# Attention's projection in two halves, its result added by ScalarE and GpSimd, and part of the layer norm's scale and shift on ScalarE

## The chip, the cores and the metric

The kernel runs on one core of a Trainium2 chip. The core has five engines that run side by side, each with its own queue of instructions, and that wait for one another through semaphores: TensorE (PE in the profile, its weight loads apart as PEld), VectorE (DVE), ScalarE (ACT), GpSimd (POOL) and SyncE (SP). Matrix products land in PSUM, a memory of eight banks; one bank holds one tile of 128 x 512 float32 numbers. Everything else lies in the larger SBUF. The metric is the time of one execution on the device in microseconds (us), the median of several runs.

## The reference, cut to what matters

The network takes an image of 256 x 256 positions with 32 channels through four layers, each a group norm, a layer and a residual addition. The change is in the first layer, attention over an axis of length one:

```
B, s, i, _ = m.shape
mn = (m - mu) * jax.lax.rsqrt(var + LN_EPS) * ln_gamma + ln_beta
v = (mn @ Wv).reshape(B, s, i, H, C)
g = jax.nn.sigmoid(mn @ Wg).reshape(B, s, i, H, C)
a = jax.nn.softmax(a, axis=2)
...
o = g * jnp.einsum('bstih,bsihc->bsihc', a, v)
o = o.reshape(B, s, i, H * C)
return o @ Wo + bo
...
x = x + _L0_conv_ref(_gn(x), ...)
```

The softmax runs over an axis of length one and is 1, so the layer is `x + (sigmoid(mn @ Wg) * (mn @ Wv)) @ Wo + bo`, with `mn` the layer norm of the group-normed image. Two edge-filter layers and a recurrent layer over 256 time steps follow.

## The kernel before

The image lies in SBUF as `xa`, 128 partitions by 64 blocks by 256 columns: four neighbouring positions of 32 channels each fill the partitions. Two blocks make a pair of 128 x 512 numbers, and there are 32 pairs. `xb` holds the layer norm's result in the same form.

The layer norm ends with a loop over the 32 pairs. For each, TensorE spreads the reciprocal deviation over the partitions into a PSUM tile `pb` (L252, the pool `ps_sp` with eight banks), VectorE multiplies the pair by it (L259), and GpSimd multiplies by `gamma4` and adds `beta4` (L260). Here a scheduler keeps the program's order on each engine; the three run as a pipeline.

Attention follows, in pools of its own: `ps_g` with four banks, `ps_v` with four. They take the PSUM of the layer norm's pools, so their first tile waits for the last reader there. The work is cut into 64 units, two for each pair: unit `u = 2i + half` of step `i` computes one half of the 256 hidden columns for pair `i`.

- `gate(u)`: four matmuls (L277), one for each of the four positions, each with 32 rows of weights and 512 columns, each into its own bank of `ps_g`; then ScalarE takes the sigmoid of each into SBUF tiles `sg` (L288).
- `value(u)`: four matmuls (L277) into the four banks of `ps_v`; then VectorE multiplies each by its `sg` into `o` (L296).
- `project(i)`: eight matmuls (L302), four for each half of the hidden columns, which sum into one bank of `ps_g`, 32 of its partitions for each position. VectorE adds this sum, the bias `bo4` and the residual in one instruction (L310), and takes the statistics for the next group norm (L311).

A float32 matmul is recorded as two instructions, so four of them stand as x8 in the trace. The four matmuls of a gate or value group use different rows of TensorE and run together.

The order on each engine is the order in which the code is written (`tc.manual_schedule`). A step has `value(2i)`, `gate(2i+1)`, `value(2i+1)`, `gate(2i+2)` and `project(i-1)`: gates are one unit ahead of values, and the projection is one step behind. A tile's matmul waits until the earlier reader of its bank is done: the ScalarE sigmoid or VectorE's addition for `ps_g`, VectorE's product for `ps_v`.

After the last step the group norm of the second layer takes the statistics together (L140), and everything later waits for that.

Of the kernel before, what the change touches and what calls it, by code (L numbers as in the profile page):

```python
# [10 lines left out]
F32 = mybir.dt.float32  # L11
AF = mybir.ActivationFunctionType
ALU = mybir.AluOpType
# [3 lines left out]
S = 256  # L17
T = 256
C = 32
J = 4  # L20
NB = T // J
P = 128
# [36 lines left out]
def net_kernel(  # L59
# [20 lines left out]
    nc = tc.nc  # L80
# [11 lines left out]
    xa = big.tile([P, NB, S], F32, name="xa")  # L92
    xb = big2.tile([P, NB, S], F32, name="xb")
# [15 lines left out]
    def per_channel(v, name):  # L109

        t = cp.tile([P, 1], F32, name=name)
        for j in range(J):
            nc.gpsimd.dma_start(out=t[j * C : (j + 1) * C, :], in_=v.rearrange("(c o) -> c o", o=1))
        return t

    gamma4 = per_channel(ln_gamma, "gamma4")
    beta4 = per_channel(ln_beta, "beta4")
    bo4 = per_channel(b_o, "bo4")
# [10 lines left out]
    wo = cp.tile([P, D // P, C], F32, name="wo")  # L129
    nc.gpsimd.dma_start(out=wo, in_=w_o.rearrange("(k p) c -> p k c", p=P))  # L130

    NST = NB // 2

    def new_stats():
        return small.tile([P, NST, nc.vector.BN_STATS_DIM], F32, name="stats")
# [24 lines left out]
    stats = new_stats()  # L160
    WL = 32
    with tc.tile_pool(name="nat", bufs=3) as natp, tc.tile_pool(
        name="ps_in", bufs=4, space=PSUM
    ) as ps_in:
        for w0 in range(0, T, WL):
# [3 lines left out]
            for b2 in range(WL // (2 * J)):  # L169
# [10 lines left out]
                dst = xa[:, blk : blk + 2, :].rearrange("p b s -> p (b s)")  # L180
# [13 lines left out]
    pairs = [(g * KS + ks, g, ks) for ks in range(KS) for g in range(4)]  # L194

    def pair(t, k):
        return t[:, 2 * k : 2 * k + 2, :].rearrange("p b s -> p (b s)")

    with tc.tile_pool(name="ln", bufs=4) as lnp:


        avg = lnp.tile([P, KS, KS, J], F32, name="avg", bufs=1)
        nc.gpsimd.memset(avg, 0.0)
        for ks in range(KS):
            nc.gpsimd.tensor_copy(avg[:, ks, ks, :], kt[:, K_AVG, 0:P:C])
        spread = lnp.tile([P, KS * J, C], F32, name="spread", bufs=1)
        for g in range(4):
            rows = slice(g * C, (g + 1) * C)
            nc.gpsimd.tensor_copy(
                spread[rows], ident[rows, rows].unsqueeze(2).to_broadcast([C, KS * J, C])  # L210
            )
        rstd = lnp.tile([P, 2 * S], F32, name="rstd", bufs=1)
        with tc.tile_pool(name="ps_ln", bufs=6, space=PSUM) as ps_ln, tc.tile_pool(
            name="ps_var", bufs=1, space=PSUM
        ) as ps_var:
            cen = lnp.tile([P, P], F32, name="cen", bufs=1)
            nc.vector.tensor_scalar(cen, kt[:, K_CEN, :], gn[0], None, ALU.mult)
            pcb = ps_var.tile([P, 1], F32, name="pcb")
            nc.tensor.matmul(pcb, lhsT=kt[:, K_CEN, :], rhs=gn[1], start=True, stop=True)
            cb = lnp.tile([P, 1], F32, name="cb", bufs=1)  # L220
            nc.vector.tensor_copy(cb, pcb)
            pvar = ps_var.tile([P, 2 * S], F32, name="pvar")
            sqs = {}

            def variance(k, g, ks):
                nc.tensor.matmul(
                    pvar[g * C : (g + 1) * C, :],
                    lhsT=avg[:, ks].rearrange("p k j -> p (k j)"),
                    rhs=sqs.pop(k),
                    start=ks == 0,  # L230
                    stop=ks == KS - 1,
                )

            for i, (k, g, ks) in enumerate(pairs):
                pc = ps_ln.tile([P, 2 * S], F32, name="pc")
                nc.tensor.matmul(pc, lhsT=cen, rhs=pair(xa, k), start=True, stop=True)
                sqs[k] = lnp.tile([P, 2 * S], F32, name="sq", bufs=10)
                nc.scalar.activation(sqs[k], pc, AF.Square, bias=cb)
                nc.vector.tensor_scalar(pair(xb, k), pc, cb, None, ALU.add)
                if g == 3 and ks:  # L240
                    for q in pairs[i - 7 : i - 3]:
                        variance(*q)
            for q in pairs[-4:]:
                variance(*q)
            std = lnp.tile([P, 2 * S], F32, name="std", bufs=1)
            nc.scalar.activation(std, pvar, AF.Sqrt, bias=ln_eps)
            nc.vector.reciprocal(rstd, std)
        with tc.tile_pool(name="ps_sp", bufs=8, space=PSUM) as ps_sp:
            for k, g, ks in pairs:
                rows = slice(g * C, (g + 1) * C)  # L250
                pb = ps_sp.tile([P, 2 * S], F32, name="pb")
                nc.tensor.matmul(  # L252
                    pb,
                    lhsT=spread[rows, ks * J : (ks + 1) * J, :].rearrange("p j c -> p (j c)"),
                    rhs=rstd[rows, :],
                    start=True,
                    stop=True,
                )
                nc.vector.tensor_mul(pair(xb, k), pair(xb, k), pb)  # L259
                nc.gpsimd.tensor_scalar(  # L260
                    pair(xb, k), pair(xb, k), gamma4, beta4, ALU.mult, ALU.add
                )

    stats = new_stats()
    with tc.tile_pool(name="at", bufs=3) as atp, tc.tile_pool(
        name="ps_g", bufs=4, space=PSUM
    ) as ps_g, tc.tile_pool(name="ps_v", bufs=4, space=PSUM) as ps_v:
        gates, gated = {}, {}  # L270

        def inner(w, u, j, ps):
            i, half = divmod(u, 2)
            k = pairs[i][0]
            rows = slice(j * C, (j + 1) * C)
            mn = xb[rows, 2 * k : 2 * k + 2, :].rearrange("p b s -> p (b s)")
            nc.tensor.matmul(  # L277
                ps, lhsT=w[rows, half * P : (half + 1) * P], rhs=mn, start=True, stop=True
            )
            return ps  # L280

        def gate(u):
            pgs = [
                inner(wg4, u, j, ps_g.tile([P, 2 * S], F32, name="pg")) for j in range(J)
            ]
            for j, pg in enumerate(pgs):
                gates[u, j] = sg = atp.tile([P, 2 * S], F32, name="sg", bufs=8)
                nc.scalar.activation(sg, pg, AF.Sigmoid)  # L288

        def value(u):  # L290
            pvs = [
                inner(wv4, u, j, ps_v.tile([P, 2 * S], F32, name="pv")) for j in range(J)
            ]
            for j, pv in enumerate(pvs):
                gated[u, j] = o = atp.tile([P, 2 * S], F32, name="o", bufs=17)
                nc.vector.tensor_mul(o, pv, gates.pop((u, j)))  # L296

        def project(i):
            po = ps_g.tile([P, 2 * S], F32, name="pg")
            for half in range(2):  # L300
                for j in range(J):
                    nc.tensor.matmul(  # L302
                        po[j * C : (j + 1) * C, :],
                        lhsT=wo[:, half, :],
                        rhs=gated.pop((2 * i + half, j)),
                        start=half == 0,
                        stop=half == 1,
                    )
            dst = pair(xa, pairs[i][0])
            nc.vector.scalar_tensor_tensor(dst, po, bo4, dst, ALU.add, ALU.add)  # L310
            nc.vector.bn_stats(stats[:, i, :], dst)  # L311

        with tc.manual_schedule():
            gate(0)
            for i in range(NST):
                value(2 * i)
                gate(2 * i + 1)
                value(2 * i + 1)
                if i + 1 < NST:
                    gate(2 * i + 2)  # L320
                if i >= 1:
                    project(i - 1)
            project(NST - 1)
    with tc.tile_pool(name="ps_gn", bufs=1, space=PSUM) as ps_gn:
        gn = group_norm(stats, ps_gn)

# [549 lines left out]
```

## Time and profile before

The time before is 3012.37 us, the median of three runs between 3011.68 and 3013.71. The profiled execution spans 3003.6 us.

| stretch of the span | us | what runs |
|---|---|---|
| 0 to 40 | 40 | load, transposes, first statistics |
| 40 to 83 | 43 | group norm, centring and variance of the layer norm |
| 88 to 108 | 20 | scale by the deviation (32 products on VectorE), scale and shift on GpSimd |
| 107.4 to 360.1 | 253 | attention |
| 360 to 655 | 295 | two edge-filter layers |
| after | 2349 | weights and recurrence |

| instruction of the trace | count | mean ns |
|---|---|---|
| L288 ScalarE, sigmoid of 128 x 512 from PSUM | 256 | 602 |
| L296 VectorE, product with `sg` from PSUM | 256 | 678 |
| L310 VectorE, sum with bias and residual | 32 | 751 |
| L311 VectorE, statistics | 32 | 694 |
| L260 GpSimd, scale and shift of 128 x 512 | 32 | 776 |

A line of the timeline has the start in us, the length in us, the engine, the source line, the operation, the tile written and the tiles read, their shapes, and how many instructions were merged; in brackets stand the idle time of the engine before and what ended it. A line of the waits has the waiting engine, tile and line, then whom it waited for, the sum in us, the number of times, and the longest. A line of the stages has the stretch, its length, each engine's busy time with the number of instructions, and the clock that TensorE was granted (1.00 is full). Ends of matmuls are modelled, so a busy TensorE may still stand idle, and instructions that follow each other closely overlap, so that 678 ns products can start 0.6 us apart.

### The profile page before, as it was taken

The numbers are of one execution on the slowest core, as the hardware profiler recorded it, in microseconds if no ns is written. First come the engines' busy times: TensorE is split into PE (matmuls) and PEld (weight loads), VectorE is DVE, ScalarE is ACT, GpSimd is POOL, SyncE is SP. The second block draws the span as 40 slices with busy tenths as digits, with TensorE's granted clock in tenths as the row PEclk, the third lists the DMA queues.
The fourth block names the chain that finished last, engine by engine and source line by source line (L and its number), as shares of the span: only waits on it lengthen the run. The fifth ranks groups of instructions, "written<-read, shape, count | busy, mean of one in ns | idle before, by whom it ended". The sixth has DMA issues, their size and how long they took to land.

```text
span 3003.6 us, 39237 instructions
## 1 busy us (share of the span) xinstructions
PE 2830.3 (94%) x10209; PEld 1042.6 (35%) x10209; DVE 2646.4 (88%) x6572; ACT 1986.9 (66%) x5393; POOL 1718.6 (57%) x2272
## 2 busy tenths in 40 slices
PE   7899898988999999999999999999999999999997
PEld 4433333332333333333333333333333333333332
DVE  5778798986999999999999999999999999999997
ACT  5355486755666666676666766676666666666665
POOL 2300055636666666666666666666666666666665
PEclk9899999988999999999999999999999999999999
DMA  3000000001000000000000000000000000000000
GB/s 128 1 1 1 1 1 1 1 15 24 11 16 8 15 9 15 8 15 8 15 8 15 8 16 7 17 15 8 16 8 15 10 16 8 16 8 15 1 8 9
DMA packets 29314, 38.42 MB, mean 13 GB/s; under 512 B 5732, under 2 KB 22149, under 8 KB 29080
## 3 DMA queue, kind: packets, MB, share of 16 engines
q1 hardware_dynamic: 27392, 33.57, 3.9%
q8 instruction: 84, 1.38, 0.2%
q10 hardware_dynamic: 888, 1.95, 0.2%
q14 instruction: 150, 1.23, 0.1%
q0 software_dynamic: 800, 0.30, 0.0%
HBM read 10.63 MB, written 8.39 MB: 6 GB/s over the span
## 4 chain that ended last, share of the span: by engine, by line
PE 42%; DVE 39%; POOL 10%; issue 4%; ACT 2%; DVEq 0%; POOLq 0%; ACTq 0%
DVE ve L731 13%; PE zz L718 11%; POOL rs L734 9%; DVE zn L738 8%; PE zz L713 7%; DVE c L759 6%; DVE c L767 6%; PE pv L277 4%; PE pt L777 4%; PE pg L440 4%; PE pg L400 3%; PE px L792 2%; PE zz L702 2%; PE pg L302 2%; DVE h L774 2%
## 5 line engine op out<-in xcount | busy, mean ns | idle before, releaser
L734 POOL TENSOR_TENSOR rs<-ve,mhalf 128x4 f32<-128x4 f32 x1024 | 1036.6, 1012 | 281.5 <-DVE ve L731 237.1
L718 PE MATMUL zz<-wc,hT 128*128 128x512 f32 x2040 | 962.6, 594 | 1.2 <-DVE hT L782 1.2
L754 ACT ACTIVATE ga<-zn 128x384 f32<-128x384 f32 x1024 | 531.3, 519 | 468.0 <-DVE zn L738 467.5
L738 DVE TENSOR_TENSOR zn<-zz,rs 128x512 f32<-128x512 f32 x1024 | 701.1, 685 | 84.7 <-POOL rs L734 76.6
L763 POOL TENSOR_TENSOR fc<-ga,c 128x128 f32<-128x128 f32 x1020 | 466.8, 458 | 522.4 <-ACT ga L754 522.4
L731 DVE TENSOR_REDUCE ve<-sq 128x4 f32<-128x516 f32 x1024 | 697.2, 681 | 16.6 <-POOL sq L669 14.1
L726 ACT ACTIVATE sq<-zz 128x512 f32<-128x512 f32 x1024 | 606.3, 592 | 26.6 <-PE zz L718 14.3
L702 PE MATMUL zz<-fx,xt 33*128 33x512 f32 x2048 | 584.8, 643 | 11.5 <-DVE zn L738 8.2
L713 PE MATMUL zz<-wc,hT 128*128 128x512 f32 x1024 | 525.3, 595 | 0.0
L718 PEld LDWEIGHTS zz<-wc,hT 128*128 128x128 f32 x2040 | 359.6, 196 | 264.6 <-DVE hT L782 213.7
L771 ACT ACTIVATE th<-c 128x128 f32<-128x128 f32 x1024 | 311.4, 304 | 182.6 <-DVE c L767 177.9
L777 PEld LDWEIGHTS pt<-ident,h 128*128 128x128 f32 x1024 | 141.9, 139 | 804.8 <-DVE h L774 710.2
L777 PE MATMUL pt<-ident,h 128*128 128x128 f32 x1024 | 321.7, 314 | 87.6 <-DVE h L774 79.2
L767 DVE TENSOR_TENSOR c<-c,fc 128x128 f32<-128x128 f32 x1020 | 291.2, 286 | 55.9 <-DVE c L759 2.3
L759 DVE TENSOR_TENSOR c<-ga 128x128 f32<-128x128 f32 x1024 | 302.9, 296 | 38.7 <-ACT ga L756 38.6
L756 ACT ACTIVATE ga<-zn 128x128 f32<-128x128 f32 x1024 | 303.2, 296 | 0.0
L774 DVE TENSOR_TENSOR h<-ga,th 128x128 f32<-128x128 f32 x1024 | 292.0, 285 | 0.8 <-ACT th L771 0.8
L702 PEld LDWEIGHTS zz<-fx,xt 33*128 33x128 f32 x2048 | 156.1, 185 | 298.4 <-PE zz L718 226.3
L288 ACT ACTIVATE sg<-pg 128x512 f32<-128x512 f32 x256 | 132.1, 602 | 110.8 <-PE pg L277 110.8
L713 PEld LDWEIGHTS zz<-wc,hT 128*128 128x128 f32 x1024 | 183.3, 219 | 2.3 <-issue 2.3
L393 POOL TENSOR_TENSOR dh<-pp 128x512 f32<-128x512 f32 x64 | 99.4, 1553 | 115.6 <-DVE pp L380 98.9
L296 DVE TENSOR_TENSOR o<-pv,sg 128x512 f32<-128x512 f32 x256 | 155.4, 678 | 4.4 <-ACT sg L288 4.1
(147 smaller groups left out, 2306.8 us busy)
## 6 DMA issues: line engine op xcount, KB each, us to landing
xt<-xa SPq DMA_DIRECT2D x256, 64.0 KB, 2.0
nat<-in_x_dram SPq DMA_DIRECT2D x16, 512.0 KB, 8.3
out_dram<-st SPq DMA_DIRECT2D x32, 256.0 KB, 2.3
wc<-in_L_conv_W_cell_dram ACTq DMA_DIRECT2D x2, 512.0 KB, 4.1
kt<-in_consts_dram ACTq DMA_DIRECT2D x1, 832.0 KB
wv<-in_L_conv_Wv_dram POOLq DMA_DIRECT2D x4, 32.0 KB, 4.8
wg<-in_L_conv_Wg_dram POOLq DMA_DIRECT2D x4, 32.0 KB, 6.6
gamma<-in_L_conv_ln_gamma_dram POOLq DMA_DIRECT2D x4, 0.1 KB, 6.1
```

Source lines behind the costliest of these rows:

```text
L702: nc.tensor.matmul(zz, lhsT=x, rhs=fx[rows, l, :], start=True, stop=l == 0 and t == 0)
L713: nc.tensor.matmul(get("zz"), lhsT=v["hT", 0, t][:, seqs], rhs=wc[:, l, 0, :], start=False, stop=t == 0)
L718: nc.tensor.matmul(get("zz"), lhsT=v["hT", l, t - 1][:, seqs], rhs=wc[:, l, 1, :], start=False, stop=True,)
L726: nc.scalar.activation(sqs[l, h][:, :, 0:H], four(get("zz")), AF.Square, scale=float(H**-0.5))
L731: nc.vector.tensor_reduce(ve, sqs[l, h], AX.X, ALU.add)
L734: nc.gpsimd.tensor_tensor(rs, get("ve"), mhalf, ALU.pow)
L738: nc.vector.tensor_mul(four(zn), four(get("zz")), get("rs").unsqueeze(2).to_broadcast([P, 4, H]))
L754: nc.scalar.activation(ga[:, 0 : 3 * H], get("zn")[:, 0 : 3 * H], AF.Sigmoid)
L759: nc.vector.tensor_mul(c, gates(get("ga"), 0), gates(get("ga"), 3))
L763: nc.gpsimd.tensor_mul(fc, gates(get("ga"), 1), get("c"))
L767: nc.vector.tensor_add(c, c, get("fc"))
L777: nc.tensor.transpose(pt[:, 0:P], get("h"), ident)
```

## The change

`project` is called twice for a step. The first call, before `value(2i+1)`, opens the sum in a bank of `ps_g` with the first half's four matmuls; the second, after `gate(2i+2)`, adds the other four. It is meant to fill TensorE between the other groups and to take work from VectorE: the finished sum goes through ScalarE, which adds the bias and writes it to an SBUF tile `r`, and GpSimd adds `r` to the residual. The statistics stay on VectorE, in a function of their own that is called three steps later, so that VectorE need not wait for GpSimd. In the layer norm, 12 of the 32 scale-and-shift operations (groups 1 and 3, where `ks % 4 < 3`) go from GpSimd to ScalarE, so that the two share them.

```diff
                 nc.vector.tensor_mul(pair(xb, k), pair(xb, k), pb)
-                nc.gpsimd.tensor_scalar(
-                    pair(xb, k), pair(xb, k), gamma4, beta4, ALU.mult, ALU.add
-                )
+                if g % 2 and ks % 4 < 3:
+                    nc.scalar.activation(
+                        pair(xb, k), pair(xb, k), AF.Identity, scale=gamma4, bias=beta4
+                    )
+                else:
+                    nc.gpsimd.tensor_scalar(
+                        pair(xb, k), pair(xb, k), gamma4, beta4, ALU.mult, ALU.add
+                    )
...
-        def project(i):
-            po = ps_g.tile([P, 2 * S], F32, name="pg")
-            for half in range(2):
-                for j in range(J):
-                    nc.tensor.matmul(
-                        po[j * C : (j + 1) * C, :],
-                        lhsT=wo[:, half, :],
-                        rhs=gated.pop((2 * i + half, j)),
-                        start=half == 0,
-                        stop=half == 1,
-                    )
-            dst = pair(xa, pairs[i][0])
-            nc.vector.scalar_tensor_tensor(dst, po, bo4, dst, ALU.add, ALU.add)
-            nc.vector.bn_stats(stats[:, i, :], dst)
+        sums = {}
+
+        def project(i, half):
+            if half == 0:
+                sums[i] = ps_g.tile([P, 2 * S], F32, name="pg")
+            for j in range(J):
+                nc.tensor.matmul(
+                    sums[i][j * C : (j + 1) * C, :],
+                    lhsT=wo[:, half, :],
+                    rhs=gated.pop((2 * i + half, j)),
+                    start=half == 0,
+                    stop=half == 1,
+                )
+            if half == 1:
+                r = atp.tile([P, 2 * S], F32, name="r", bufs=2)
+                nc.scalar.activation(r, sums.pop(i), AF.Identity, bias=bo4)
+                dst = pair(xa, pairs[i][0])
+                nc.gpsimd.tensor_add(dst, dst, r)
+
+        def statistics(i):
+            nc.vector.bn_stats(stats[:, i, :], pair(xa, pairs[i][0]))
 
         with tc.manual_schedule():
             gate(0)
             for i in range(NST):
                 value(2 * i)
                 gate(2 * i + 1)
+                if i >= 3:
+                    statistics(i - 3)
+                if i >= 1:
+                    project(i - 1, 0)
                 value(2 * i + 1)
                 if i + 1 < NST:
                     gate(2 * i + 2)
                 if i >= 1:
-                    project(i - 1)
-            project(NST - 1)
+                    project(i - 1, 1)
+            for half in range(2):
+                project(NST - 1, half)
+            for i in range(NST - 3, NST):
+                statistics(i)
```

## The prediction

> **What bounds the kernel now.** I read the slices first (TensorE at 9 tenths nearly throughout), then the stages. Attention, from the first value group of step 1 to the start of the last step:
>
> ```profile
> core 0: us, PE busy (x) PEld busy (x) DVE busy (x) ACT busy (x) POOL busy (x), PEclk, DMA share, GB/s
> 123.03:349.72 226.69, 220.97 (x1396) 87.11 (x1392) 180.28 (x290) 119.78 (x232) 0.00 (x0) 1.00 0.00 1
> ```
>
> These are 29 steps, so 226.69/29 = 7.82 us a step. VectorE is busy for 180.28/29 = 6.2 us of it, GpSimd not at all. TensorE looks full, but modelled matmul ends hide its gaps, so I took the waits of the same stretch:
>
> ```profile
> ACT sg L288 <- PE pg L277: 107.0, 58, 2.5
> PEld pv L277 <- DVE o L296: 56.3, 116, 1.0
> DVE xa L310 <- PE pg L302: 47.0, 30, 1.6
> PEld pg L302 <- ACT sg L288: 22.0, 29, 0.8
> ```
>
> Each engine waits for the next in a ring: value matmuls for VectorE's products (their four banks), the projection for a sigmoid (its bank), VectorE for the projection, ScalarE for gates. No engine is full; the length of the ring counts. One step in order of time:
>
> ```profile
> 201.20 1.14 PE L277 MATMUL pv<-xb,wv 32*128 32x512 f32 x8
> 202.16 1.10 PE L277 MATMUL pg<-xb,wg 32*128 32x512 f32 x8
> 202.74 4.86 DVE L296 TENSOR_TENSOR o<-pv,sg 128x512 f32<-128x512 f32 x8
> 203.22 2.06 ACT L288 ACTIVATE sg<-pg 128x512 f32<-128x512 f32 x4 [2.48 <-PE pg L277]
> 203.46 2.48 PE L277 MATMUL pv<-xb,wv 32*128 32x512 f32 x7 [0.20 <-DVE o L296]
> 205.36 0.85 PE L277 MATMUL pg<-xb,wg 32*128 32x512 f32 x3
> 206.49 2.07 ACT L288 ACTIVATE sg<-pg 128x512 f32<-128x512 f32 x4 [1.21 <-PE pg L277]
> 207.16 1.92 PE L302 MATMUL pg<-o,wo 128*32 128x512 f32 x16
> 209.02 0.71 PE L277 MATMUL pv<-xb,wv 32*128 32x512 f32 x4
> ```
>
> I call the groups A (values of 2i, 201.20), B (gates of 2i+1, 202.16), D (values of 2i+1, from 203.46), E (gates of 2i+2, 205.36) and the projection (207.16); the next A is at 209.02. D's tiles come one by one, 0.6 apart, as the products free their banks, and E starts only behind the last, although sigmoids of B had freed banks from 203.8 on: TensorE holds program order. The projection waits for the first sigmoid of E.
>
> **What the Trainium skill says.** "TensorEngine Tiling (Array Packing)", Key Properties: changing the tiling mode drains TensorE. The trace agrees, cheaply. The weight loads of the projection, and of the last step's single value tile before a projection, show it:
>
> ```profile
> 207.16 0.16 PEld L302 LDWEIGHTS pg<-o,wo 128*32 128x32 f32 x8 [0.76 <-ACT sg L288]
> 207.62 0.13 PEld L302 LDWEIGHTS pg<-o,wo 128*32 128x32 f32 x4 [0.30 <-issue]
> 208.05 0.13 PEld L302 LDWEIGHTS pg<-o,wo 128*32 128x32 f32 x4 [0.30 <-issue]
> ```
>
> ```profile
> 353.77 0.29 PEld L277 LDWEIGHTS pv<-xb,wv 32*128 32x128 f32 x2 [0.30 <-DVE o L296]
> 354.82 0.16 PEld L302 LDWEIGHTS pg<-o,wo 128*32 128x32 f32 x8 [0.76 <-issue]
> ```
>
> The projection's four passes are 0.43 to 0.46 apart, and from the last (208.48) to A it is 0.54. "GPSIMD Engine Reference", 4.1 Engine selection: GpSimd can't read PSUM and takes about twice VectorE's time on two inputs. Here the 128x512 add to `sh` (L389) takes 1036 ns there and the subtraction to `dh` (L393) 1553, against VectorE's 678 for a product. "SBUF — State Buffer", two separate sides: VectorE and GpSimd exclude one another when VectorE has two SBUF inputs or a 2-port mode. The attention products read one PSUM and one SBUF operand, so I expect no collision; the layer norm, of the same form, shows none (678 ns beside busy GpSimd). "ScalarE: Activation LUTs", What ACT_TABLE_LOAD costs: a pointer bias gives 280 + 0.833 N ns, 707 ns as an estimate for 512. The trace has 687 (L238, from PSUM with a bias), which I use.
>
> **The layer norm's scale and shift.** 12 of the 32 go to ScalarE. In the trace:
>
> ```profile
> 88.15 19.22 DVE L259 TENSOR_TENSOR xb<-xb,pb 128x512 f32<-128x512 f32 x32 [2.16 <-PE pb L252]
> 89.04 24.08 POOL L260 TENSOR_SCALAR xb<-xb,gamma,beta 128x512 f32<-128x512 f32 x32 [49.44 <-DVE xb L259]
> 109.59 1.28 ACT L288 ACT_TABLE_LOAD   x1 [26.99 <-PE pg L277]
> ```
>
> GpSimd runs to 113.1, VectorE to 107.37, and attention's first gate starts at 107.44. The page names GpSimd as its releaser, but as built this gate needs only GpSimd's first pair, and VectorE's last product, which frees the PSUM of the old pool. Later gates need later pairs, all done in time. GpSimd's 12 x 0.75 = 9 us were behind the front and are worth 0; ScalarE was idle for 27 us, so its 12 x 0.80 (L364, 801 ns, two pointers) are hidden too, and the table load waits for the first gate as before.
>
> **The projection in two parts.** From VectorE go one 0.75 us addition a step from PSUM and the wait of up to 1.6 us for it; the statistics stay, three steps late. ScalarE gets one `r` a step (602 ns, a sigmoid, to 707; I take 687), GpSimd one add (1.04 to 1.55). In 8 us both are small: ScalarE 4.13 + 0.69, GpSimd at most 1.55. VectorE falls to 6.2 - 0.75, about 5.5.
>
> What matters is where the halves stand. The order on TensorE becomes A, B, C (first half of step i-1), D, E, F (second half). The gates and the sum share four banks of `ps_g`, and now the sum holds one from C to F. In the program as built:
> - C waits for B's first sigmoid: B holds all four banks.
> - E finds three free banks. Its fourth tile takes the one that E's own first sigmoid frees, so F and everything behind queue on TensorE for a round trip through ScalarE.
> - B's fourth tile waits for `r`.
>
> A step from these pieces, A's start at 0:
> - B at 0.96 (202.16 - 201.20).
> - B's first sigmoid 1.06 later (203.22 - 202.16), at 2.02; it takes 0.60, and TensorE answers 0.07 later (207.09 to 207.16): C at 2.69. B's matmuls are issued by 1.82, so TensorE idles 0.87.
> - C has two passes of the old projection's four, 0.46 + 0.54 with the switch: D at 3.69. VectorE, no longer held by addition and statistics, starts A's products at about 1.19 (0.07 after the second pass), 0.6 apart; the last ends at 3.66, so D's tiles go together. E at 4.65 (0.96, like A to B). Before it was at 4.16: 0.49 lost.
> - E's first sigmoid at 5.71, done 6.31, fourth tile at 6.36. One tile and the switch take 1.05 (353.77 to 354.82): F at 7.41. Two passes: next A at 8.41. From E's sigmoid to the next A that is 2.70; before it was 2.53 (206.49 to 209.02): 0.17 lost. E to its sigmoid takes 0.07 less (1.06, not 1.13).
> - `r` starts 0.1 after the next A and ends at 0.8, ahead of B's fourth tile at 0.99: hidden. VectorE's last product starts at 6.7 and ends at 7.3: hidden, with 2.9 us idle.
>
> So 8.40 for 7.82, +0.58 a step. Steps 1 to 30 have both halves: 30 x 0.58 = 17.4. In the last step the old tail from A (349.72) to the aggregate (360.12) took 10.4. Now D's last product ends at 7.35, F's passes at 8.46, `r` at 9.2, the add at 10.3 to 10.8, the statistics at 11.0 to 11.5: +0.7 to +1.2, I take 0.8. Sum 18.2; 3012.4 + 18.2 = 3030.6.
>
> **The rivals.**
> - *Faster, the ring opens.* If neither bank wait came last, a step would be TensorE's groups end to end: 4 x 0.96 + 2 x 1.00 = 5.84 (VectorE's 5.5 lies under it), 2.0 less x 31 = 61 us, 2951. For: VectorE sheds work and its 1.6 us wait. Against: the built waits and only four banks.
> - *Faster, one bank wait binds.* Without E's round trip F would follow E by about 1.05: A at 4.65 + 1.05 + 1.00 = 6.70, 2978. Without C's wait D would be paced by the products to about 3.7 and E start near 3.8, the rest as above: 7.56, 3004. Each needs a free bank that I can't find.
> - *Same.* A step within 0.2 of 7.82: my round trips would have to be over by 0.2 each. They are the measured ones.
> - *Slower still.* If `r` came late to B's fourth tile, the add collided with VectorE, or the granted clock fell below 1.00 in longer gaps: 8.8 a step, +30, 3043.
>
> **How the numbers follow.** My case 0.75, slower still 0.09, same 0.04, ring open 0.04, one wait 0.08. Errors of 0.1 on each of the two round trips and on the switches give 8.1 to 8.7, so +9 to +28. The range 3016 to 3041 leaves out the faster cases and a part of the slowest. Chances: faster 0.12, same 0.04, slower 0.84.
>
> **What would show it.** A step of about 8.4 us; the first weight load of the projection waiting about 0.9 for a sigmoid; a single `pg` tile 1.7 us behind the first of its group, released by ScalarE, then the second half; `pv` tiles no longer waiting 0.3 for products; VectorE idle some 2.9 us a step, waiting for `pv`; the first gate still near 107.4. It is wrong if a step takes under 7.8, if the fourth gate tile of E goes with its group, or if the layer norm's end moves the first gate.

## The result, and the profile after

The changed kernel takes 3027.97 us (median of four runs, 3022.59 to 3032.14) beside 3012.02 for the kernel before: a ratio of 1.0051, 95% interval 1.0032 to 1.0071. It is slower by 16 us; 18.2 were forecast. In the two profiles, from attention's first gate to the aggregate of its statistics, 252.7 us (107.44 to 360.12) became 271.2 (105.16 to 376.37): 18.5 more. The rest of the span gives 1.4 of it back: attention starts 2.3 earlier (107.44 to 105.16), and what follows it takes 0.8 longer. The earlier start is not the edit's: VectorE's products of the layer norm begin 2.3 earlier too (88.15 to 85.86), ahead of the first edited operation, and in the ten profiles of this case that beginning lies anywhere from 85.9 to 88.2.

The changed kernel numbers its lines anew: gates and values are L282 (L277 before), the sigmoid L293 (L288), the product L301 (L296), the projection L309 (L302). `r` is L318, GpSimd's addition L320, the statistics L323. The letters A to F are those of the prediction. A stretch of about 28 steps, engine by engine:

```profile
core 0: us, PE busy (x) PEld busy (x) DVE busy (x) ACT busy (x) POOL busy (x), PEclk, DMA share, GB/s
121.50:356.20 234.70, 198.71 (x1352) 61.77 (x1344) 155.35 (x251) 138.09 (x253) 35.48 (x28) 1.00 0.00 1
```

A step takes 8.37 us (from one A, at 205.90 below, to the next, at 214.27), up from 7.82. VectorE's work fell from 6.2 to 155.35/28 = 5.5 us a step, as intended, yet the step grew: VectorE's busy time did not set it. The waits of the same stretch:

```profile
DVE o L301 <- PE pv L282: 79.1, 56, 2.2
PEld pg L282 <- ACT sg L293: 42.0, 28, 1.5
PEld pg L309 <- ACT sg L293: 40.3, 28, 1.5
PEld pv L282 <- DVE o L301: 23.5, 28, 0.8
```

VectorE now waits 2.8 us a step for TensorE, in two gaps (2.2 and 0.6). Before, its only wait of size was for the projection (1.6). The second line is new, and the third has grown from 0.8: in each of 28 steps TensorE's weight loads wait 1.5 us for a sigmoid at a gate tile, and 1.4 at the first half of the projection. The step, first TensorE and then ScalarE:

```profile
205.90 1.14 PE L282 MATMUL pv<-xb,wv 32*128 32x512 f32 x8
206.86 1.10 PE L282 MATMUL pg<-xb,wg 32*128 32x512 f32 x8
208.56 1.06 PE L309 MATMUL pg<-o,wo 128*32 128x512 f32 x8 [0.61 <-ACT sg L293]
209.56 1.23 PE L282 MATMUL pv<-xb,wv 32*128 32x512 f32 x8
210.52 1.03 PE L282 MATMUL pg<-xb,wg 32*128 32x512 f32 x6
212.22 1.12 PE L282 MATMUL pg<-xb,wg 32*128 32x512 f32 x2 [0.67 <-ACT sg L293]
213.27 1.06 PE L309 MATMUL pg<-o,wo 128*32 128x512 f32 x8
214.27 0.71 PE L282 MATMUL pv<-xb,wv 32*128 32x512 f32 x4
```

```profile
206.09 0.69 ACT L318 ACTIVATE r<-pg,bo 128x512 f32<-128x512 f32 x1 [0.49 <-PE pg L309]
207.91 2.06 ACT L293 ACTIVATE sg<-pg 128x512 f32<-128x512 f32 x4 [1.13 <-PE pg L282]
211.57 1.58 ACT L293 ACTIVATE sg<-pg 128x512 f32<-128x512 f32 x3 [1.60 <-PE pg L282]
213.38 0.60 ACT L293 ACTIVATE sg<-pg 128x512 f32<-128x512 f32 x1 [0.23 <-PE pg L282]
```

The gate group E has broken in two: x6 at 210.52 (three tiles) and x2 at 212.22 (the fourth), 1.70 later, just after the sigmoid that began at 211.57 ended (the first of the three in that line, 0.6 long). The second half of the projection and the next value group stand behind it. Likewise the first half, at 208.56, starts only after the sigmoid that began at 207.91.

### The profile page after: what moved, and what is told of

Read it like the earlier page. It is cut to its first block, busy times and chain, and to the rows that moved or that the text cites. A ratio compares the mean times of both kernels' runs of the same rounds, so it can differ in the third digit from the quotient of the medians.

```text
span 3020.7 us, 39322 instructions
## 1 busy us (share of the span) xinstructions
PE 2814.8 (93%) x10209; PEld 1016.2 (34%) x10209; DVE 2627.7 (87%) x6540; ACT 2020.4 (67%) x5437; POOL 1746.3 (58%) x2292
## 4 chain that ended last, share of the span: by engine, by line
PE 44%; DVE 38%; POOL 10%; issue 4%; ACT 3%; DVEq 0%; POOLq 0%; ACTq 0%
DVE ve L750 13%; PE zz L737 11%; POOL rs L753 9%; DVE zn L757 8%; PE zz L732 7%; DVE c L778 6%; DVE c L786 6%; PE pg L459 4%; PE pt L796 4%; PE pg L419 4%; PE pg L282 3%; PE px L811 2%; PE pv L282 2%; PE zz L721 2%; PE pg L309 2%
## 5 line engine op out<-in xcount | busy, mean ns | idle before, releaser
L301 DVE TENSOR_TENSOR o<-pv,sg 128x512 f32<-128x512 f32 x256 | 158.9, 684 | 91.0 <-PE pv L282 86.8
L293 ACT ACTIVATE sg<-pg 128x512 f32<-128x512 f32 x256 | 135.3, 602 | 90.0 <-PE pg L282 90.0
L320 POOL TENSOR_TENSOR xa<-xa,r 128x512 f32<-128x512 f32 x32 | 40.5, 1267 | 228.7 <-ACT r L318 228.7
```

## The experiments

The theory: four banks of `ps_g` now hold a half-done sum across a gate group, and the two waits for a sigmoid that follow are the loss (the bank theory). The rivals: the route by ScalarE and GpSimd costs; the switches of tiling mode, twice as many, cost; the layer norm's edit costs. In the diffs `-` is the changed kernel unless it says otherwise. Time ratios are to the kernel before, with 95% intervals.

**The layer norm's edit alone** (`ln_alone`), on the kernel before:

```diff
+                if g % 2 and ks % 4 < 3:
+                    nc.scalar.activation(pair(xb, k), pair(xb, k), AF.Identity, scale=gamma4, bias=beta4)
+                else:
                     nc.gpsimd.tensor_scalar(pair(xb, k), pair(xb, k), gamma4, beta4, ALU.mult, ALU.add)
```

> The kernel before with only the layer norm's 12 scale-and-shift operations on ScalarE. Bank theory: nothing, within 2 us of before (3012), the first gate of attention still starts 0.1 us after VectorE's last product of the layer norm, and a step of attention stays at 7.82 us. Rival, the layer norm's edit costs part of the 16 us: 3 us or more over before.

Measured: 3011.54 us, ratio 1.0002 (0.9993 to 1.0011). In its timeline VectorE's last product ends at 86.40 + 19.21 = 105.61, and the first gate starts at 105.72:

```profile
86.40 19.21 DVE L259 TENSOR_TENSOR xb<-xb,pb 128x512 f32<-128x512 f32 x32 [2.16 <-PE pb L252]
105.72 2.09 PE L282 MATMUL pg<-xb,wg 32*128 32x512 f32 x8 [2.76 <-POOL xb L265]
```

So the gate keeps 0.1 behind VectorE's last product, as before (107.37 and 107.47), and a step stays at 7.82. The bracket names GpSimd, but GpSimd's last operations run on to 106.95, after the gate has started. This edit is worth nothing that shows; the interval leaves about 3 us either way.

**The new route, with the projection whole** (`whole_new_add`):

```diff
-                if i >= 1:
-                    project(i - 1, 0)
                 value(2 * i + 1)
                 if i + 1 < NST:
                     gate(2 * i + 2)
                 if i >= 1:
-                    project(i - 1, 1)
+                    for half in range(2):
+                        project(i - 1, half)
```

> The changed kernel with the projection in one piece again, after the second gate group; the sum still goes by ScalarE and GpSimd, the statistics still come three steps late. Bank theory: the route by ScalarE and GpSimd is a gain by itself. VectorE starts on the value tiles at 1.19 us after their group, not 1.54, the second value group ends 0.35 earlier, and a step takes 7.47 us: 30 x -0.35 + 0.9 at the end = 3002. Rival, the route by ScalarE and GpSimd is what costs: the step stays at 8.3 or so, 3025 to 3028.

Measured: 3003.18 us, ratio 0.9977 (0.9969 to 0.9986), faster than before. Its timeline, from one whole projection to the next:

```profile
204.54 1.92 PE L309 MATMUL pg<-o,wo 128*32 128x512 f32 x16
206.40 1.14 PE L282 MATMUL pv<-xb,wv 32*128 32x512 f32 x8
207.63 2.48 DVE L301 TENSOR_TENSOR o<-pv,sg 128x512 f32<-128x512 f32 x4 [2.06 <-PE pv L282]
212.07 1.92 PE L309 MATMUL pg<-o,wo 128*32 128x512 f32 x16
```

A step is 212.07 - 204.54 = 7.53 (7.47 expected), and VectorE starts 1.23 after the value group where it started 1.54 after it before (201.20 to 202.74). The route by ScalarE and GpSimd, with the statistics moved back, is a gain of 0.3 us a step. The rival falls.

**The halves, with VectorE's addition as before** (`split_old_add`):

```diff
-                r = atp.tile([P, 2 * S], F32, name="r", bufs=2)
-                nc.scalar.activation(r, sums.pop(i), AF.Identity, bias=bo4)
                 dst = pair(xa, pairs[i][0])
-                nc.gpsimd.tensor_add(dst, dst, r)
+                nc.vector.scalar_tensor_tensor(dst, sums.pop(i), bo4, dst, ALU.add, ALU.add)
+                nc.vector.bn_stats(stats[:, i, :], dst)
```

(The separate statistics go.)

> The changed kernel with VectorE's addition and statistics as before, and the projection still in two halves. Bank theory: the halves alone make the loss, and who adds is hidden: a step of 8.4 us, 3026 to 3029, like the changed kernel. Rival, the route by ScalarE and GpSimd costs: back to 3012.

Measured: 3029.13 us, ratio 1.0064 (1.0048 to 1.0081).

```profile
206.73 1.14 PE L282 MATMUL pv<-xb,wv 32*128 32x512 f32 x8
208.26 2.47 DVE L301 TENSOR_TENSOR o<-pv,sg 128x512 f32<-128x512 f32 x4
209.39 1.07 PE L309 MATMUL pg<-o,wo 128*32 128x512 f32 x8 [0.60 <-ACT sg L293]
213.05 1.12 PE L282 MATMUL pg<-xb,wg 32*128 32x512 f32 x2 [0.67 <-ACT sg L293]
215.10 1.14 PE L282 MATMUL pv<-xb,wv 32*128 32x512 f32 x8
```

The step is 215.10 - 206.73 = 8.37, the changed kernel's. VectorE is back to a start 1.53 after the value group, and it makes no difference. With the two runs before it this completes the square: whole and old addition 7.82, whole and new 7.53, halves and old 8.37, halves and new 8.37. The halves are the loss, and they also hide the gain of the new route.

**The second half ahead of the gate group** (`second_half_first`):

```diff
+                if i >= 1:
+                    project(i - 1, 1)
                 if i + 1 < NST:
                     gate(2 * i + 2)
-                if i >= 1:
-                    project(i - 1, 1)
```

> The changed kernel with one exchange: the second half of the projection stands before the second gate group, so that the sum's bank is closed before that group needs four. As many mode switches, the same instructions. Bank theory: the group's fourth tile now waits for ScalarE's result r of the sum, about 0.9 us, and only value tiles stand behind it, which are paced by VectorE anyway; a step of 6.7 us, 30 x -1.1 + 0.9 = 2980. Rival, the switches of tiling mode on TensorE make the loss: still 8.4 us a step, 3028.

Measured: 3000.38 us, ratio 0.9967 (0.9954 to 0.9979). The same instructions, halves and mode switches in another order take the step from 8.37 to 7.39: the switches are not the loss, the sum's bank held across a gate group is. The size was wrong; I expected 6.7. A part of TensorE's weight loads, from one first half of the projection to the next:

```profile
206.80 0.16 PEld L309 LDWEIGHTS pg<-o,wo 128*32 128x32 f32 x8 [0.76 <-ACT sg L293]
207.79 0.31 PEld L282 LDWEIGHTS pv<-xb,wv 32*128 32x128 f32 x8 [0.84 <-DVE stats L323]
208.87 0.16 PEld L309 LDWEIGHTS pg<-o,wo 128*32 128x32 f32 x8 [0.76 <-issue]
212.16 0.29 PEld L282 LDWEIGHTS pg<-xb,wg 32*128 32x128 f32 x2 [0.20 <-ACT sg L293]
212.65 0.29 PEld L282 LDWEIGHTS pg<-xb,wg 32*128 32x128 f32 x2 [0.20 <-ACT sg L293]
213.14 0.29 PEld L282 LDWEIGHTS pg<-xb,wg 32*128 32x128 f32 x2 [0.20 <-ACT sg L293]
214.19 0.16 PEld L309 LDWEIGHTS pg<-o,wo 128*32 128x32 f32 x8 [0.76 <-ACT sg L293]
```

The step is 214.19 - 206.80 = 7.39. B's tiles come 0.49 apart as the sigmoids of E free their banks, so a new ring is closed: E, its four sigmoids, B's last tile at 213.14, then 1.05 for this one tile and the switch. The expectation has no such ring: it speaks of E's fourth tile and the value tiles behind it, and not of B's tiles waiting in turn.

**Five banks for gates and sum** (`five_gate_banks`):

```diff
-        name="ps_g", bufs=4, space=PSUM
-    ) as ps_g, tc.tile_pool(name="ps_v", bufs=4, space=PSUM) as ps_v:
+        name="ps_g", bufs=5, space=PSUM
+    ) as ps_g, tc.tile_pool(name="ps_v", bufs=3, space=PSUM) as ps_v:
```

> The changed kernel with one bank moved from the value tiles (4 to 3) to the gates and the sum (4 to 5). The sum then finds a free bank, and the second gate group finds four: both new waits for a sigmoid go. But the fourth value tile of each group waits for the product of the first of its own group, with the sum's halves queued behind. Bank theory: the ring of the gates is only exchanged for one of the values, 9.7 us a step, 3012 + 31 x 1.85 = 3068. Rival, the two waits for a sigmoid are the whole loss: 3012 or less.

Measured: 3075.15 us, ratio 1.0208 (1.0189 to 1.0226).

```profile
204.67 1.13 PE L282 MATMUL pv<-xb,wv 32*128 32x512 f32 x6
205.90 2.67 DVE L301 TENSOR_TENSOR o<-pv,sg 128x512 f32<-128x512 f32 x4 [1.61 <-PE pv L282]
206.64 0.69 PE L282 MATMUL pv<-xb,wv 32*128 32x512 f32 x1 [0.84 <-DVE o L301]
206.75 0.70 PE L282 MATMUL pg<-xb,wg 32*128 32x512 f32 x3
211.52 0.69 PE L282 MATMUL pv<-xb,wv 32*128 32x512 f32 x1 [0.84 <-DVE o L301]
214.43 1.13 PE L282 MATMUL pv<-xb,wv 32*128 32x512 f32 x6
```

Now the value group breaks (x6, then the fourth tile 1.97 later behind VectorE's first product), and the gates come together. It happens twice a step (206.64, 211.52), and a step takes 214.43 - 204.67 = 9.76 (9.7 expected). A fifth bank cures both sigmoid waits, but the group that lost the bank pays more. As the bank had to come from the values, this run does not say what the two waits cost by themselves.

**The projection whole, in the middle** (`whole_in_the_middle`):

```diff
                 if i >= 1:
-                    project(i - 1, 0)
+                    for half in range(2):
+                        project(i - 1, half)
                 value(2 * i + 1)
                 if i + 1 < NST:
                     gate(2 * i + 2)
-                if i >= 1:
-                    project(i - 1, 1)
```

> The changed kernel with the projection in one piece between the first gate group and the second value group: value, gate, projection, value, gate. The second gate group has four banks again, and two mode switches a step go. Bank theory: the ring is then second value group, its four products, the next value group, first gate tile, its sigmoid, projection: 7.4 us a step, 3001. Rival, the mode switches are what counts: 0.4 us less than the 7.39 of the exchange run, 7.0 a step, 2988.

Measured: 3000.82 us, ratio 0.9967 (0.9954 to 0.9979).

```profile
204.72 1.10 PE L282 MATMUL pg<-xb,wg 32*128 32x512 f32 x8
205.73 2.48 PE L282 MATMUL pv<-xb,wv 32*128 32x512 f32 x7
209.43 1.92 PE L309 MATMUL pg<-o,wo 128*32 128x512 f32 x16
212.25 1.09 PE L282 MATMUL pg<-xb,wg 32*128 32x512 f32 x8
```

A step is 212.25 - 204.72 = 7.53 (7.4 expected). Two switches fewer a step than in the exchange run (`second_half_first`), and no shorter step: no sign that the switches cost. On TensorE this is the round of `whole_new_add` (two value groups, each followed by a gate group, and one whole projection), begun one unit later, so the two share their 7.53, and one value group still takes 2.48, paced by VectorE's products.

**The gate group ahead of the value group** (`gates_first`), an edit of the last run:

```diff
-                value(2 * i)
                 gate(2 * i + 1)
+                value(2 * i)
```

> Like the run with the projection in the middle, and the first gate group ahead of the first value group: gate, value, projection, value, gate. Bank theory: the first gate group now waits for the sigmoids of the second alone and no longer stands behind value tiles that VectorE frees one by one; 7.1 us a step, 2993. Rival, no order helps further because TensorE's passes bind: no better than the run with the projection in the middle.

Measured: 3018.45 us, ratio 1.0024 (1.0014 to 1.0034), far from the 2993 expected: 217.61 - 209.71 = 7.90 a step.

```profile
209.71 1.92 PE L309 MATMUL pg<-o,wo 128*32 128x512 f32 x16
214.23 2.16 PE L282 MATMUL pg<-xb,wg 32*128 32x512 f32 x6 [0.61 <-ACT sg L293]
215.70 0.70 PE L282 MATMUL pv<-xb,wv 32*128 32x512 f32 x2
216.24 1.44 PE L282 MATMUL pv<-xb,wv 32*128 32x512 f32 x5
217.61 1.92 PE L309 MATMUL pg<-o,wo 128*32 128x512 f32 x16
```

Two gate groups now follow each other. The value tiles stand in line behind the last gate tile, which comes at 215.70, when the last sigmoid of the group before frees its bank, and the last value tile uses the same rows of TensorE as that gate tile. From 215.70 to the projection it is 1.91, nearly twice the 1.05 of a lone tile and its switch; that the two tiles queue for their rows fits this, and was not tested apart. In the other orders a value group stands between the two gate groups.

**The changed kernel once more** (`after_again`), unedited.

> The changed kernel once more, beside the others: 8.4 us a step, 3022 to 3032, slower than before by 0.3 to 0.7 per cent. It tells nothing apart; it narrows the interval and shows another profile of the same program.

Measured: 3026.39 us, ratio 1.0053 (1.0037 to 1.0070). Attention takes 271.2 us in its profile (105.56 to 376.77), as in the first.

The exchange run and the projection in the middle, both at 0.9967, beat the kernel before by 10 to 11 us and the changed kernel by about 26. They are not equal in attention: from the first gate to the aggregate it takes 241.7 us in the exchange run (106.84 to 348.50), 247.9 in the other (106.64 to 354.55), and 246.5 in `whole_new_add` (106.84 to 353.37). Of the 6 us between the first two, 4 lie in 29 steps of 7.39 and 7.53. By attention itself the exchange run is the best; what comes after attention hides it.

## Why the prediction was right

It forecast +18.2 us by a step of 8.40; measured are +16 and 8.37, and +18.5 in attention itself: 16.2 in the 29 steps from A of step 2 to A of the last, 1.4 ahead of them and 1.0 behind. (The stretch that the prediction divides by 29 begins with step 2, counted from 0, not with step 1; the division is right.) By its own steps, with A's start (205.90) as 0:

- *B and its sigmoid.* Expected at 0.96 and 2.02; in the trace 0.96 and 2.01.
- *C behind B's first sigmoid.* Expected 2.69, measured 2.66 (208.56). D 3.69, measured 3.66. The sign given for this wait was off: the first weight load of C waits 1.44, not 0.9, because B's weight loads are done by 1.22, where the working had B issued by 1.82. It waits for the same sigmoid, so C's start is unchanged.
- *E and its fourth tile.* E at 4.62 (4.65 expected), its sigmoid at 5.67 (5.71), the fourth tile at 6.32 (6.36), F at 7.37 (7.41), the next A at 8.37 (8.41). E comes 0.46 later than the old 4.16, and from its sigmoid to the next A it takes 2.70 where it took 2.53, as the working had it.
- *The route by ScalarE and GpSimd.* `r` took 687 ns, as taken from L238; GpSimd's add 1267, inside the range of 1036 to 1553. VectorE's products took 684 ns on average, from 678 before and 681 in `split_old_add`, where GpSimd adds nothing. No collision shows, which agrees with the Trainium skill, "SBUF — State Buffer", Who interferes with whom: a VectorE instruction with at most one SBUF input, outside the 2-port modes, does not contend with GpSimd. `r` had less room than thought: it starts 0.19 after A, not 0.1, and ends at 0.88, where B's tiles go at 0.96; one weight load of B waits 0.2 for it. Hidden, but barely; the whole step stays as it is in `split_old_add`, which has no `r`.
- *The layer norm at nothing.* Shown by `ln_alone`. The first gate came at 105.16, not near 107.4, but again 0.1 behind VectorE's last product (85.86 + 19.22 = 105.08); that it came earlier has its origin ahead of the edit.
- *The end.* From the last step's A to the aggregate 376.37 - 365.01 = 11.36, for 10.40: +0.96, where +0.8 was taken.

The rivals: the ring did not open, since both bank waits stand in the trace; "same" and "slower still" fall with the step's length.

That the sum's bank, held across a gate group, is the cause is shown by order alone in `second_half_first`, and the square of four runs, with `ln_alone`, shows that nothing else in the edit costs. How the loss divides between the two waits (0.46 ahead of E, 0.17 behind its sigmoid, less 0.08 between the two) is read from the traces; no run took away one of them and left everything else.

That the +16 is smaller than attention's +18.5 goes with the spread between executions of one kernel. The changed kernel's first four lie between 3022.6 and 3032.1 us, and the kernel before, over all its comparisons, between 3004.0 and 3014.1; the times go with TensorE's granted clock, averaged over the execution. Where both are known:

| mean granted clock | before | changed |
|---|---|---|
| 0.980 or 0.981 | 3004.0 to 3006.5 | 3022.6 to 3026.9 |
| 0.977 | 3010.2 to 3013.7 | 3031.3 to 3032.1 |

At a like clock the change costs about 19 us, an estimate from the middles of these ranges. The +16 sets two executions of the first row and two of the second against four of before at 3010.9 or more, whose clock is not known. At least part of the spread lies behind attention, where all ten kernels have the same code: from the aggregate to the end their profiles take 2643.5 to 2644.5 us at a mean clock of 0.979 or more, and 2645.2 to 2652.1 at 0.977 or 0.978. In attention's steady steps the clock was 0.99 or 1.00 in all of them. Why it differs between executions stays open.

## What to carry to other kernels

Before splitting an accumulation to fill gaps, count the PSUM banks that it keeps while other groups run: a group of four tiles that finds three banks turns its last tile into a round trip through the engine that empties the first, with everything behind it in TensorE's order waiting. Where every engine has slack, add up the ring of waits instead of the busy times; 0.7 us less work on VectorE was worth 0.3 us in one order and nothing in another. When working out a paced group, give its last tile its own passes on the rows that it shares: in the two experiments that fell short of their expectation most, such a tile stood 1.05 and 1.91 us ahead of the projection. And compare the stretch that an edit changes in the profiles, beside the whole time: here 6 us between two orders were hidden in the rest.

## What the runs showed that was not expected

- A single tile of a row-tiled group costs TensorE about as much as four: 1.05 us to the next tiling mode (212.22 to 213.27), where a full group takes 1.08 (207.79 to 208.87 in `second_half_first`). A straggler is therefore worth a whole group.
- The better orders close rings of their own. In `second_half_first` two groups of four gate tiles go through four banks, each emptied by sigmoids 0.49 apart, at 7.39 us a step; with the projection whole, a value group waits for VectorE's products, 0.6 apart, at 7.53. The prediction's estimate for TensorE's groups end to end, 5.84 with four switches, stayed out of reach of every order tried.
